# Layer 0 of a four-layer kernel: ten chunks of x turned twice instead of stored and loaded back

## The chip, the cores and the metric

The kernel runs on one core of a Trainium2 chip. The core has a matrix engine (TensorE, "PE" in the profile; "PEld" is its weight load), a vector engine (VectorE, DVE), an activation engine (ScalarE, ACT), a general engine (GpSimd, POOL) and a queue engine (SyncE, SP) that here only issues transfers. Each engine runs its own instruction stream in order; semaphores tie the streams together. SBUF is the on-chip memory of 128 partitions; PSUM is the small memory that TensorE writes into, eight banks of 512 fp32 values in each partition; transfers (DMA) go between SBUF and device memory (DRAM). The metric is the device time of one execution in microseconds. Everything is fp32.

## The reference, cut to what matters

Four residual layers on x of shape (1, 256, 256, 128), that is 65536 tokens of 128 channels. Each is `x = x + f(_gn(x))`, where `_gn` is a group norm whose means run over all tokens. Only the start of layer 0 is touched: the group statistics, and the LayerNorm row factors and the triangle bias that attention needs.

```python
def _gn(v, G=32, eps=1e-5):                      # mean and variance over all tokens and 4 channels
    g = v.reshape(B_, H_, W_, G, C_ // G)
    m = jnp.mean(g, axis=(1, 2, 4), keepdims=True)
    s = jnp.var(g, axis=(1, 2, 4), keepdims=True)
    return ((g - m) / jnp.sqrt(s + eps)).reshape(v.shape)

def _L0_conv_ref(x, mask, ...):                  # x is _gn(x) here
    xn = (x - mu) * jax.lax.rsqrt(var + EPS) * ln_w + ln_b        # LayerNorm of each token
    tri_bias = jnp.einsum('bijd,dh->bhij', xn, w_tri)[:, None]
    q, k, v = ...                                                  # xn @ w_q, w_k, w_v, 4 heads of 32
    scores = jnp.einsum('bimhc,binhc->bihmn', q, k) + tri_bias + mask_bias
    o = jnp.einsum('bihmn,binhc->bimhc', jax.nn.softmax(scores, axis=-1), v)
    return (sigmoid(xn @ w_g + b_g) * o) @ w_o + b_o

x = x + _L0_conv_ref(_gn(x), ...)
```

The bias `tri_bias` is shared by all rows of the attention, so attention can't start before every token of x has been through the LayerNorm sums, and these need the group statistics of all tokens first. So x is passed over twice before attention begins.

## The kernel before

x is cut into 32 chunks of 2048 tokens (`SC`, `NSC`), 1 MiB each. The input has tokens along the rows (`x_tok`); the layers want channels on the partitions (`xT`, a DRAM scratch tensor), so each chunk is turned by TensorE.

**First stage** (L262 to L380). `load0(i)` issues the load of the i-th chunk of `order0` into a buffer `p0_x` on SP. Three such buffers, and three more borrowed for the first six loads, bound how far it runs ahead: inside the loop the load of chunk i+3 is issued when chunk i has been turned. For each half of a chunk, 8 transposes go into a PSUM tile `p0_t` of two banks (L359), two `bn_stats` on VectorE sum it (L361), and ScalarE copies it to SBUF (L366), regrouping the tokens. Chunks 0 to 13 (`HELD` = 14) stay in SBUF; chunks 14 to 31 go to three buffers `p0_xc` and from there by SP to `xT` (L375). Of these, 14 to 16 (`FRESH` = 3) are the last three to use the buffers, and are still there at the end. `order0` is 17 to 31, 14 to 16, 0 to 13. From the seventh chunk on, each chunk also runs one step of `folds()`, small weight products on TensorE and VectorE that use weights loaded by POOL. Behind the last chunk but one comes an aggregate of all sums so far (`gn_part`, L380 and L181), behind the last one the small chain to the group mean and deviation (`gn_merge`, `gn_groups`).

**Second pass** (L437 to L592), order written out by hand (`manual_schedule`: program order is the order on every engine). Over `order` = 14, 15, 16, 0, 1, 2, 3, 17, 4, 18, 5, ... : `rows1(i)` squares the chunk on ScalarE (L452) and multiplies it by `wt` on TensorE (L455): four pieces of 512 tokens, each into its own 32 of the 128 columns of the array and so side by side. `squares1(i-1)` adds the products of the squares to the same PSUM tile (L463), and VectorE evicts it (L468). `turn1(i-2)` turns the evicted rows with four transposes (L476) into `p1_pt`, which has two buffers, and `keep1(i-2)` copies them to `raw` (L480). `marks` says at which iteration the variance, root and normalization of finished rows are done. `fetch()` issues the load of a stored chunk from `xT` into one of the three buffers (L396), and `keep()` the store of a held chunk to `xT` (L403): eight halves before the pass, the others at each iteration that uses a fetched chunk. At iterations 11 and 20 to 27 the first rows, loads and projections of attention are put in between (`first_rows`, `load_x`, `load_rs`, `first_qk`, `first_v`). PSUM is full: three banks for `p1_pr`, two for `p1_pt`, three for the pool `psP` of those small products.

**Attention** (from L598) then loads groups of 1024 tokens from `xT` and runs most of the first half of the span; nothing of it is changed.

Of the kernel before, what the change touches and what calls it, by code (L numbers as in the profile page):

```python
# [8 lines left out]
F32 = mybir.dt.float32  # L9
# [6 lines left out]
P = 128  # L16
# [15 lines left out]
def kernel(ctx: ExitStack, tc: tile.TileContext, a: dict, out: bass.AP):  # L32
# [214 lines left out]
    with tc.tile_pool(name="x0", bufs=1, reuse_waits="tile") as xres, tc.tile_pool(name="p0", bufs=3, reuse_waits="tile") as sb:  # L247
# [3 lines left out]
        def hold(s):  # L251
            if s < 4:
                held[s] = tuple(gt_tile(f"x0_{s}_{h}", *tags[2 * s + h]) for h in range(2))
            elif s < 9:
                tile_ = att_sb.tile([P, 2, GT], F32, name=f"x0_{s}", tag="qk" if s < 6 else "vg", bufs=2 if s < 6 else 3)
                held[s] = tile_.rearrange("p a t -> p (a t)")
            else:
                held[s] = xres.tile([P, SC], F32, name=f"x0_{s}")
            return held[s]

        order0 = [*range(HELD + FRESH, NSC), *range(HELD, HELD + FRESH), *range(HELD)]
        with tc.tile_pool(name="p0ps", bufs=3, space=PSUM, reuse_waits="tile") as ps, tc.tile_pool(name="f0ps", bufs=2, space=PSUM, reuse_waits="tile") as fps, tc.tile_pool(name="f0", bufs=1, reuse_waits="tile") as wk, tc.manual_schedule():  # L262
            xts, loaded = {}, {}

# [87 lines left out]
            nc.sync.dma_start(mk, a["L0_conv_mask"].rearrange("b (t p) n -> p (b t) n", p=P))  # L352
            for i, s in enumerate(order0):
                xt = xts.pop(s)
                xc = hold(s) if s < HELD else sb.tile([P, SC], F32, name="p0_xc", tag="xs")
                for c in range(2):
                    pt = ps.tile([P, 8, P], F32, name="p0_t")
                    for k in range(8):
                        nc.tensor.transpose(pt[:, k, :], xt[:, c, k, :], ident)  # L359
                    for h in range(2):  # L360
                        nc.vector.bn_stats(  # L361
                            stats0[:, i * 4 + 2 * c + h, :],
                            pt[:, 4 * h : 4 * h + 4, :].rearrange("p k n -> p (k n)"),
                        )
                    xh = xc[c] if isinstance(xc, tuple) else xc[:, c * GT : (c + 1) * GT]
                    nc.scalar.copy(  # L366
                        xh.rearrange("p (n k) -> p n k", k=8),
                        pt.rearrange("p k n -> p n k"),
                    )
                if i < 3:  # L370
                    load0(i + 6)
                elif i > 5:
                    load0(i + 3)
                if s not in held:
                    nc.sync.dma_start(xT[:, s * SC : (s + 1) * SC], xc)  # L375
                    loaded[s] = xc
                if i >= 6:
                    next(steps, None)
                if i == NSC - 2:
                    mv_first = gn_part(stats0, 0, T // CK - 4, "gn0_a")  # L380
# [1 line left out]


        fresh = range(HELD, HELD + FRESH)
        order = [*fresh, *range(4)]
        for i in range(HELD - 4):
            order += [HELD + FRESH + i, 4 + i]
        order += range(HELD + FRESH + HELD - 4, NSC)
        to_load, to_store = [s for s in order if s not in held and s not in fresh], list(held)
        loaded = {s: loaded[s] for s in fresh}  # L390

        def fetch():
            if to_load:
                s = to_load.pop(0)
                loaded[s] = sb.tile([P, SC], F32, name="p1_xc", tag="xs")
                nc.sync.dma_start(loaded[s], xT[:, s * SC : (s + 1) * SC])  # L396

        def keep():
            if to_store:
# [2 lines left out]
                    at += s * SC  # L402
                    nc.sync.dma_start(xT[:, at : at + xh.shape[-1]], xh)  # L403

        for _ in range(8):
            keep()
        mv0 = gn_merge(
            mv_first, gn_part(stats0, T // CK - 4, T // CK, "gn0_b"), 1.0 - 4.0 * CK / T, "gn0_mv"
# [25 lines left out]
        nc.vector.tensor_scalar(woh, wo, 0.5 * SHIFT, None, ALU.mult)  # L434


        with tc.tile_pool(name="p1", bufs=3, reuse_waits="tile") as wk_sb, tc.tile_pool(name="p1ps", bufs=3, space=PSUM, reuse_waits="tile") as ps, tc.tile_pool(name="p1pt", bufs=2, space=PSUM, reuse_waits="tile") as psT, tc.tile_pool(name="p1mm", bufs=3, space=PSUM, reuse_waits="tile") as psP:  # L437
# [3 lines left out]
            pw = psP.tile([P, 1], F32, name="p1_pw", tag="mm")  # L441
            for c in range(4):
                nc.tensor.matmul(pw[32 * c : 32 * c + 32, :], lhsT=mw, rhs=ones[:, 0:1], start=True, stop=True)
            nc.vector.tensor_copy(off, pw)
            with tc.manual_schedule():
                prs, trs, turned, sqs = {}, {}, {}, {}

                def rows1(i):
                    xc = held[order[i]] if order[i] in held else loaded[order[i]]
                    sqs[i] = sb.tile([P, SC], F32, name="p1_sq", tag="xt")  # L450
                    for at, xh in spans(xc):
                        nc.scalar.activation(sqs[i][:, at : at + xh.shape[-1]], xh, AF.Square, bias=mrneg, scale=r0)  # L452
                    prs[i] = ps.tile([P, CK], F32, name="p1_pr")
                    for c in range(4):
                        nc.tensor.matmul(  # L455
                            prs[i][32 * c : 32 * c + 32, :], lhsT=wt, rhs=piece(xc, c), start=True, stop=False
                        )

                def squares1(i):
                    pr = prs.pop(i)  # L460
# [40 lines left out]
                    )  # L501

                def first_rows():
                    pt = psP.tile([P, 2, P], F32, name="p1_rs", tag="mm")
# [30 lines left out]
                def first_qk():  # L535
                    tiles(0)
                    t = groups[0]
                    for j, what in enumerate("qk"):
                        pm = psP.tile([P, CK], F32, name="p1_mm", tag="mm")
                        nc.tensor.matmul(pm, lhsT=wf[:, j * D : (j + 1) * D], rhs=t["xn"][:, 0:CK], start=True, stop=True)  # L540
                        if j:
                            nc.vector.tensor_scalar(t["k"][:, 0:CK], pm, cqkg[:, 1:2], None, ALU.add)
                        else:
                            nc.vector.tensor_scalar(t["q"][:, 0:CK], pm, cqkg[:, 0:1], qscale, ALU.add, ALU.mult)

                def first_v():
                    t = groups[0]
                    pm = psP.tile([P, CK], F32, name="p1_mm", tag="mm")
                    for k in range(4):
                        nc.tensor.matmul(  # L550
                            pm[:, k * D : (k + 1) * D], lhsT=t["xn"][:, k * P : (k + 1) * P],
                            rhs=wf[:, 2 * D : 3 * D], start=True, stop=True,
                        )
                    nc.vector.tensor_tensor(t["v"][:, 0:4, :], pm.rearrange("p (k d) -> p k d", d=D), cv, ALU.add)

                qscale = 1.0 / float(HC) ** 0.5
                marks = {8: [(0, 4)], 17: [(4, 8), (14, 21)], 24: [(8, 12), (21, 25)], 29: [(12, 14), (25, 28)]}
                for i in range(NSC + 2):
                    if i < NSC:
                        rows1(i)  # L560
# [1554 lines left out]
```

## Time and profile before

| what | value |
|---|---|
| median of 3 runs | 3225.62 us (3222.66 to 3227.78) |
| the profiled execution, its own time | 3230.19 us |
| its span in the trace | 3228.1 us |
| mean granted TensorE clock | 0.973 |
| busy over the span: PE, DVE, ACT, POOL | 95%, 70%, 63%, 54% |
| first stage | 0 to 153.4 us |
| second pass, to attention's first scores | 153.4 to 244.2 us |
| moved by DMA in the first 140.3 us | 53.71 MB |
| moved by DMA from 153 to 247 us | 27.94 MB |

How to read it: the two stages changed take 7.6% of the span, and the whole-span shares say nothing about them; each stage is read from its own windows. A row of the timeline gives the start in us from the span's start, the busy time, the engine, the line of the kernel, the operation with the tiles that it writes and reads, how many instructions are merged into it, and in brackets how long the engine stood idle before and what ended that. A matrix product of fp32 shows as two records, so four products are x8. A row of a group gives busy time, mean ns of one, and the idle time before them with its releasers. The granted clock is the share of full speed that the throttle gave TensorE. DMA share is the mean busy share of the core's 16 DMA engines; it can come out a little over 1.

### The profile page before, as it was taken

The page shows a single profiled execution, that of the slowest core. Times are in us where ns is not written, and L with a number is a line of the kernel's source. Part 1 is how long each engine was busy: PE and PEld are TensorE (multiplying, and loading weights), DVE is VectorE, ACT ScalarE, POOL GpSimd, SP SyncE. Part 2 cuts the span into 40 slices and gives each one's busy share as a digit, 9 for nine tenths or more (in the row PEclk, how much of TensorE's full clock was granted, in tenths as well). Part 3 has the DMA queues.
Part 4 walks back from the last instruction along what each step waited for, and adds up shares of the span by engine and source line. Part 5 has one row for each costly group of instructions (what it writes and reads, how often), then busy time and mean ns, then how long its engine had stood idle before and what let it go on. Part 6 is the DMA issues. An engine that isn't in the chain of part 4 may idle for free. (4 is left out here: it accounts for less than half of the span.)

```text
span 3228.1 us, 51744 instructions
## 1 busy us (share of the span) xinstructions
PE 3052.8 (95%) x19916; PEld 1633.6 (51%) x19916; DVE 2260.7 (70%) x2631; ACT 2035.8 (63%) x2276; POOL 1741.9 (54%) x955
## 2 busy tenths in 40 slices
PE   5699999999999999998798899999999999979998
PEld 4535555555555555552533344444699943324444
DVE  5657888888888888884456454445455578867887
ACT  3577777777777777764477544444344457767776
POOL 4006777777777777772277000000255568848887
PEclk8899999999999999999899899999999999989999
DMA  9982333333333333349689677676699989986885
GB/s 377 397 302 96 110 123 114 106 114 118 113 112 120 113 107 116 118 149 418 190 306 390 248 294 301 238 266 257 262 351 351 351 332 387 386 287 198 236 236 156
DMA packets 289239, 746.16 MB, mean 231 GB/s; under 512 B 68314, under 2 KB 138860, under 8 KB 240700
## 3 DMA queue, kind: packets, MB, share of 16 engines
q1 hardware_dynamic: 276561, 716.84, 62.0%
q0 software_dynamic: 9136, 24.01, 2.0%
q8 instruction: 159, 2.61, 0.3%
q10 hardware_dynamic: 3288, 1.93, 0.2%
q14 instruction: 95, 0.77, 0.1%
HBM read 455.24 MB, written 287.45 MB: 230 GB/s over the span
## 5 line engine op out<-in xcount | busy, mean ns | idle before, releaser
L679 POOL TENSOR_TENSOR p_es<-p_e 128x1024 f32<-128x1024 f32 x256 | 603.1, 2366 | 319.0 <-DMA p_x<-xT 195.3
L669 DVE TENSOR_TENSOR p_e<-p_S,tri_raw 128x1024 f32<-128x1024 f32 x512 | 609.3, 1212 | 143.4 <-PE p_S L659 143.3
L677 ACT ACTIVATE p_e<-p_e,mbT 128x1024 f32<-128x1024 f32 x512 | 552.1, 1138 | 62.1 <-DVE p_e L669 62.0
L1273 PE MATMUL p_pm<-p_zn,wf 128*128 128x512 f32 x1040 | 450.4, 595 | 1.9 <-ACT p_a L1339 1.9
L644 PE MATMUL p_mm<-p_xn,w 128*128 128x512 f32 x764 | 404.4, 612 | 0.0
L1273 PEld LDWEIGHTS p_pm<-p_zn,wf 128*128 128x128 f32 x1040 | 197.4, 190 | 255.0 <-issue 248.1
L659 PE MATMUL p_S<-p_qk 32*128 32x256 f32 x4096 | 295.4, 400 | 3.3 <-DVE p_e L669 3.3
L1407 POOL MEMSET k<- 128x512 f32 x1 | 0.5, 526 | 517.1 <-PE p_pm L1273 517.1
L659 PEld LDWEIGHTS p_S<-p_qk 32*128 32x128 f32 x4096 | 186.0, 184 | 159.2 <-PE p_mm L635 91.7
L2073 PE MATMUL tp_z<-p_B,tp_at 128*128 128x256 f32 x1024 | 250.5, 388 | 1.1 <-DVE tp_at L2064 1.1
L692 PE MATMUL p_o<-p_e,p_vg 128*32 128x256 f32 x4096 | 248.8, 383 | 0.0
L626 POOL TENSOR_TENSOR p_xn<-p_xn,p_rs 128x1024 f32<-128x1024 f32 x62 | 148.9, 2401 | 180.8 <-DMA p_rb<-rzD 99.4
L1438 POOL TENSOR_TENSOR k<-k,p_sq 128x512 f32<-128x512 f32 x128 | 163.0, 1274 | 134.4 <-ACT p_sq L1436 134.3
L2073 PEld LDWEIGHTS tp_z<-p_B,tp_at 128*128 128x128 f32 x1024 | 185.3, 191 | 23.4 <-DVE tp_at L2064 1.9
L1437 DVE TENSOR_TENSOR k<-tp_z,k 128x512 f32<-128x512 f32 x128 | 88.5, 692 | 127.5 <-ACT p_sq L1436 127.5
L644 PEld LDWEIGHTS p_mm<-p_xn,w 128*128 128x128 f32 x764 | 125.1, 190 | 103.6 <-issue 87.3
L692 PEld LDWEIGHTS p_o<-p_e,p_vg 128*32 128x32 f32 x4096 | 120.4, 110 | 110.4 <-ACT p_vg L650 41.5
L650 ACT ACTIVATE p_vg<-p_mm,bgh 128x512 f32<-128x512 f32 x128 | 88.0, 687 | 135.0 <-PE p_mm L644 135.0
L1434 ACT COPY p_K<-tp_z 128x512 f32<-128x512 f32 x128 | 75.1, 586 | 155.3 <-PE tp_z L2073 155.3
L1343 DVE SCALAR_TENSOR_TENSOR p_b<-p_pm,b2w,p_b 128x1024 f32<-128x1024 f32 x64 | 82.2, 1284 | 125.2 <-PE p_pm L1273 111.2
L635 PEld LDWEIGHTS p_mm<-w,p_xn 128*128 128x128 f32 x1016 | 133.8, 192 | 61.3 <-issue 60.6
L648 ACT ACTIVATE p_qk<-p_mm,cqkg 128x512 f32<-128x512 f32 x127 | 87.5, 689 | 122.5 <-PE p_mm L644 122.2
(429 smaller groups left out, 6087.7 us busy)
## 6 DMA issues: line engine op xcount, KB each, us to landing
p_x<-x2T SPq DMA_DIRECT2D x57, 1024.0 KB
x<-x1T SPq DMA_DIRECT2D x47, 1024.0 KB
p_x<-in_x_dram SPq DMA_DIRECT2D x32, 1024.0 KB
p_x<-xT SPq DMA_DIRECT2D x64, 512.0 KB
p_rs<-rsD SPq DMA_DIRECT2D x64, 512.0 KB
x2T<-x SPq DMA_DIRECT2D x32, 1024.0 KB
aD<-p_a SPq DMA_DIRECT2D x32, 1024.0 KB
bD<-p_b SPq DMA_DIRECT2D x32, 1024.0 KB
```

Of the source, the lines that this page charges most:

```text
L626: nc.gpsimd.tensor_tensor(xn, xn, groups[g]["rs"], ALU.mult)
L635: nc.tensor.matmul(pm[:, k * D : (k + 1) * D], lhsT=t["xn"][:, b * P : (b + 1) * P], rhs=wf[:, 2 * D : 3 * D], start=True, stop=True,)
L644: nc.tensor.matmul(pm, lhsT=w, rhs=t["xn"][:, cs_], start=True, stop=True)
L659: nc.tensor.matmul(Ss[h // 2][:, h % 2, u, :], lhsT=t["k"][hp, r * N + u * P : r * N + (u + 1) * P], rhs=t["q"][hp, r * N : (r + 1) * N], ...
L669: nc.vector.tensor_tensor(e[:, :, 2 * p : 2 * p + 2, :].rearrange("p u h n -> p h u n"), Ss[p], triT[:, 2 * p : 2 * p + 2, :, :], ALU.add,)
L677: nc.scalar.activation(e[:, u, :, :], e[:, u, :, :], AF.Exp, bias=mbT[:, u, i : i + 1])
L679: nc.gpsimd.tensor_tensor(es, e[:, 0, :, :], e[:, 1, :, :], ALU.add)
L692: nc.tensor.matmul(t["o"][hp, r % 2, :], lhsT=t["v"][:, r * 2 + u, hp], rhs=e[:, u, h, :], start=(u == 0), stop=(u == 1),)
L1273: nc.tensor.matmul(pm[:, c, :], lhsT=wf2[:, i, :], rhs=zns[s][:, k * CK : (k + 1) * CK], start=True, stop=True)
L1437: nc.vector.tensor_tensor(k1, pz, k1, ALU.add)
L1438: nc.gpsimd.tensor_tensor(k2, k2, sq, ALU.add)
L2073: nc.tensor.matmul(pz[:, t, :], lhsT=at[:, u, t * P : (t + 1) * P], rhs=Bc[:, u, :], start=(u == 0), stop=(u == 1))
```

## The change

Ten chunks, 17 to 26 (`redo`), are no longer copied or stored in the first stage: they are loaded, turned and summed only. In the second pass they are loaded again from x, turned a second time by the new `remake(i + 1)` at the end of the iteration before their own, copied to SBUF (first half by ScalarE, second by VectorE), and stored to `xT` from there. `order0` mixes two such chunks with one of the stored chunks 27 to 31, and then the fresh with the held ones; `folds()` starts at the 11th chunk. The last five held chunks (9 to 13, `late`) are used right after the fresh ones and stored before the pass; their five buffers (`x0_9` to `x0_13`) then take the fetched chunks. Fetches and keeps have fixed iterations, `marks` and the attention pieces are moved, `p1_pt` has one buffer, and a pool of two tiles of two banks (`room()`) serves the second turning and the small products.

```diff
-                held[s] = xres.tile([P, SC], F32, name=f"x0_{s}")
+                held[s] = xres.tile([P, SC], F32, name=f"x0_{s}", tag=f"x0_{s}")
...
-        order0 = [*range(HELD + FRESH, NSC), *range(HELD, HELD + FRESH), *range(HELD)]
+        redo = range(HELD + FRESH, NSC - 5)
+        order0 = []
+        for k in range(5):
+            order0 += [*redo[2 * k : 2 * k + 2], NSC - 5 + k]
+        order0 += [14, 0, 1, 2, 3, 4, 15, 5, 6, 7, 8, 9, 16, 10, 11, 12, 13]
...
-                xc = hold(s) if s < HELD else sb.tile([P, SC], F32, name="p0_xc", tag="xs")
+                xc = None
+                if s not in redo:
+                    xc = hold(s) if s < HELD else sb.tile([P, SC], F32, name="p0_xc", tag="xs")
...
+                    if s in redo:
+                        continue
                     xh = xc[c] if isinstance(xc, tuple) else xc[:, c * GT : (c + 1) * GT]
                     nc.scalar.copy(
...
-                if s not in held:
+                if s not in held and s not in redo:
                     nc.sync.dma_start(xT[:, s * SC : (s + 1) * SC], xc)
                     loaded[s] = xc
-                if i >= 6:
+                if i >= 10:
                     next(steps, None)
...
-        order = [*fresh, *range(4)]
-        for i in range(HELD - 4):
-            order += [HELD + FRESH + i, 4 + i]
-        order += range(HELD + FRESH + HELD - 4, NSC)
-        to_load, to_store = [s for s in order if s not in held and s not in fresh], list(held)
+        late = range(HELD - 5, HELD)
+        order = [*fresh, *late]
+        for i in range(HELD - 5):
+            order += [i, HELD + FRESH + i]
+        order += range(HELD + FRESH + HELD - 5, NSC)
+        to_load, to_store = [*range(HELD + FRESH, NSC)], [*late, *range(HELD - 5)]
+        fetch_at = [5, 6, 7, 8, 9, 9, 11, 13, 15, 17, 19, 21, 23, 25, 26]
+        keep_at = [1, 2, 3, 4, 6, 8, 10, 12, 14]
...
         def fetch():
...
-                loaded[s] = sb.tile([P, SC], F32, name="p1_xc", tag="xs")
-                nc.sync.dma_start(loaded[s], xT[:, s * SC : (s + 1) * SC])
+            s = to_load.pop(0)
+            k = (s - HELD - FRESH) % 5
+            x = xres.tile([P, SC], F32, name="p1_x", tag=f"x0_{late[k]}")
+            if s in redo:
+                loaded[s] = x.rearrange("p (c k d) -> p c k d", c=2, d=D)
+                nc.sync.dma_start(
+                    loaded[s], x_tok[s * SC : (s + 1) * SC, :].rearrange("(c p k) d -> p c k d", p=P, k=8)
+                )
+            else:
+                loaded[s] = x
+                nc.sync.dma_start(x, xT[:, s * SC : (s + 1) * SC])
...
-        for _ in range(8):
+        for _ in late:
             keep()
...
-        with ... tc.tile_pool(name="p1pt", bufs=2, space=PSUM ...) as psT, tc.tile_pool(name="p1mm", bufs=3, space=PSUM ...) as psP:
+        with ... tc.tile_pool(name="p1pt", bufs=1, space=PSUM ...) as psT, tc.tile_pool(name="p1x", bufs=2, space=PSUM ...) as psX:
+            def room():
+                return psX.tile([P, 8, P], F32, name="p1_t")
...
+                def remake(i):
+                    s = order[i]
+                    if s in redo:
+                        x = loaded[s]
+                        loaded[s] = sb.tile([P, SC], F32, name="p1_xc", tag="xs")
+                        for c in range(2):
+                            pt = room()
+                            for k in range(8):
+                                nc.tensor.transpose(pt[:, k, :], x[:, c, k, :], ident)
+                            (nc.vector.tensor_copy if c else nc.scalar.copy)(
+                                loaded[s][:, c * GT : (c + 1) * GT].rearrange("p (n k) -> p n k", k=8),
+                                pt.rearrange("p k n -> p n k"),
+                            )
+                        nc.sync.dma_start(xT[:, s * SC : (s + 1) * SC], loaded[s])
...
-                marks = {8: [(0, 4)], 17: [(4, 8), (14, 21)], 24: [(8, 12), (21, 25)], 29: [(12, 14), (25, 28)]}
+                marks = {9: [(9, 17)], 17: [(0, 4), (17, 21)], 26: [(4, 9), (21, 25)], 29: [(25, 28)]}
                 for i in range(NSC + 2):
+                    for at in fetch_at:
+                        if i == at:
+                            fetch()
+                    if i in keep_at:
+                        keep()
                     if i < NSC:
                         rows1(i)
-                        if order[i] not in held:
-                            fetch()
-                            if i > 1:
-                                keep()
                     if i > 1:
                         turn1(i - 2)
                     if 0 < i <= NSC:
                         squares1(i - 1)
                     if i > 1:
                         keep1(i - 2)
+                    if i + 1 < NSC:
+                        remake(i + 1)
...
-                    if i == 11:
+                    if i == 20:
                         first_rows()
-                    if i == 20:
                         load_x(0)
+                    if i == 22:
                         load_rs(0)
-                    if i == 22:
+                    if i == 24:
                         normal_x(0)
                         load_x(1)
-                    if i == 24:
+                    if i == 25:
                         load_rs(1)
-                    if i == 26:
+                    if i == 27:
                         first_qk()
-                    if i == 27:
+                    if i == 28:
                         normal_x(1)
                         first_v()
```

More of the change, by code (lines that the diff above doesn't have):

```diff
@@ L384 @@
         fresh = range(HELD, HELD + FRESH)
-        order = [*fresh, *range(4)]
-        for i in range(HELD - 4):
-            order += [HELD + FRESH + i, 4 + i]
-        order += range(HELD + FRESH + HELD - 4, NSC)
-        to_load, to_store = [s for s in order if s not in held and s not in fresh], list(held)
+        late = range(HELD - 5, HELD)
[6 more added lines that the diff above has]
+        keep_at = [1, 2, 3, 4, 6, 8, 10, 12, 14]
         loaded = {s: loaded[s] for s in fresh}
         def fetch():
-            if to_load:
-                s = to_load.pop(0)
-                loaded[s] = sb.tile([P, SC], F32, name="p1_xc", tag="xs")
-                nc.sync.dma_start(loaded[s], xT[:, s * SC : (s + 1) * SC])
+            s = to_load.pop(0)
[9 more added lines that the diff above has]
+                nc.sync.dma_start(x, xT[:, s * SC : (s + 1) * SC])
         def keep():
@@ L434 @@
         nc.vector.tensor_scalar(woh, wo, 0.5 * SHIFT, None, ALU.mult)
-        with tc.tile_pool(name="p1", bufs=3, reuse_waits="tile") as wk_sb, tc.tile_pool(name="p1ps", bufs=3, space=PSUM, reuse_waits="tile") as ps, tc.tile_pool(name="p1pt", bufs=2, space=PSUM, reuse_waits="tile") as psT, tc.tile_pool(name="p1mm", bufs=3, space=PSUM, reuse_waits="tile") as psP:
+        with tc.tile_pool(name="p1", bufs=3, reuse_waits="tile") as wk_sb, tc.tile_pool(name="p1ps", bufs=3, space=PSUM, reuse_waits="tile") as ps, tc.tile_pool(name="p1pt", bufs=1, space=PSUM, reuse_waits="tile") as psT, tc.tile_pool(name="p1x", bufs=2, space=PSUM, reuse_waits="tile") as psX:
+            def room():
+                return psX.tile([P, 8, P], F32, name="p1_t")
             mw = wk_sb.tile([P, 32], F32, name="p1_mw", bufs=1)
             nc.vector.tensor_scalar(mw, wt, mneg, None, ALU.mult)
-            pw = psP.tile([P, 1], F32, name="p1_pw", tag="mm")
+            pw = room()[:, 0, 0:1]
             for c in range(4):
@@ L503, in first_rows @@
                 def first_rows():
-                    pt = psP.tile([P, 2, P], F32, name="p1_rs", tag="mm")
+                    pt = room()[:, 0:2, :]
                     for u in range(2):
@@ L538, in first_qk @@
                     for j, what in enumerate("qk"):
-                        pm = psP.tile([P, CK], F32, name="p1_mm", tag="mm")
+                        pm = room()[:, 0:4, :].rearrange("p k d -> p (k d)")
                         nc.tensor.matmul(pm, lhsT=wf[:, j * D : (j + 1) * D], rhs=t["xn"][:, 0:CK], start=True, stop=True)
@@ L547, in first_v @@
                     t = groups[0]
-                    pm = psP.tile([P, CK], F32, name="p1_mm", tag="mm")
+                    pm = room()[:, 0:4, :].rearrange("p k d -> p (k d)")
                     for k in range(4):
```

## The prediction

> **What bounds it now.** First the busy time by windows, to see which resource is full in each stage of layer 0. Columns: window, its length, busy us (and instructions) of PE, PEld, DVE, ACT, POOL, then granted clock, DMA share, GB/s.
>
> ```profile
> 20.00:103.00 83.00, 53.94 (x313) 48.17 (x312) 49.73 (x95) 34.92 (x36) 24.86 (x47) 0.78 1.02 406
> 103.00:136.00 33.00, 23.74 (x161) 21.05 (x160) 24.46 (x40) 19.78 (x20) 0.00 (x0) 0.84 0.96 375
> 120.00:140.00 20.00, 15.44 (x120) 12.95 (x119) 19.01 (x32) 15.38 (x16) 0.00 (x0) 0.99 1.02 390
> 161.00:204.00 43.00, 42.73 (x342) 14.10 (x338) 19.06 (x47) 35.09 (x23) 0.00 (x0) 1.00 0.95 373
> ```
>
> The first stage is held by transfers (share 0.96 to 1.02, PE half idle). The second pass is held by TensorE: 42.73 busy of 43.00, while the transfers, though also near full, keep nobody waiting there. Next the timeline where the stages meet, for what lies between the last loads and the second pass.
>
> ```profile
> 140.30 1.94 PE L359 MATMUL p_t<-ident,p_x 128*128 128x128 f32 x16 [1.33 <-DMA p_x<-in_x_dram]
> 143.93 3.52 DVE L181 BATCH_NORM_AGGREGATE gn_a<-stats 128x2 f32<-128x744 f32 x1
> 147.36 2.42 DVE L361 BATCH_NORM_STATS2 stats<-p_t 128x6 f32<-128x512 f32 x4
> 153.38 6.06 ACT L452 ACTIVATE p_sq<-p_xc,mrneg,gn_rstd 128x2048 f32<-128x2048 f32 x3 [0.47 <-DVE mrneg L414]
> ```
>
> The chunk before the last lands at 140.30; its sums, the 3.52 us aggregate and the last chunk's sums follow without a gap, and 13.1 us later the second pass begins. So that landing sets the end of the stage. Then one iteration of the second pass:
>
> ```profile
> 174.87 0.66 PE L476 MATMUL p_pt<-ident,p_tr 128*128 128x128 f32 x4
> 175.46 1.07 PE L463 MATMUL p_pr<-p_sq,slide 128*32 128x512 f32 x8
> 176.34 1.04 PE L455 MATMUL p_pr<-p_xc,wt 128*32 128x512 f32 x8
> 176.59 0.75 DVE L468 TENSOR_SCALAR p_tr<-p_pr,off 128x512 f32<-128x512 f32 x1 [1.61 <-PE p_pr L463]
> 177.26 0.25 DVE L480 COPY tri_raw<-p_pt 128x96 f32<-128x96 f32 x1
> 177.40 0.66 PE L476 MATMUL p_pt<-ident,p_tr 128*128 128x128 f32 x4
> ```
>
> PE goes round in 2.53 us: turns 0.59 to the next start, squares 0.88, row products 1.06. The last is 0.18 over the equal work of the squares: the turn at 177.40 waits for the eviction that ends at 177.34. Last, the prices of the moved work, from the timeline and the groups by form:
>
> ```profile
> 131.50 1.94 PE L359 MATMUL p_t<-ident,p_x 128*128 128x128 f32 x16 [0.76 <-DMA p_x<-in_x_dram]
> 135.19 1.01 ACT L366 COPY x<-p_t 128x1024 f32<-128x1024 f32 x1 [0.18 <-PE p_t L359]
> L285 DVE COPY mbT<-f_mk 128x512 f32<-128x512 f32 x1 | 0.7, 675 | 0.0
> L480 DVE COPY tri_raw<-p_pt 128x96 f32<-128x96 f32 x32 | 7.9, 248 | 0.6 <-PE p_pt L476 0.6
> ```
>
> **Stage 1: what goes.** Up to the landing at 140.30 the queues moved 53.7 MB: 31 loads and 18 stores of 1.05 MB, and some 2.3 MB of weights. Afterwards only chunks 14 to 16 and 27 to 31 are stored, and the store of 16 is issued behind the load of the chunk before the last: 7 stores instead of 18, 11.5 MB less. At 406 GB/s that is 28.4 us. Ends: 33 if the hole of 375 against 406 also closes, 22 if two holes of 3 us open, because a load is issued only when the transposes three chunks earlier are done, and no backlog of stores then feeds the queue. I take 28.5, nearest to the longest row. VectorE does not become the bound: 20 sums took 12.30 us in a dense run, 2.46 us a chunk; from 16.5 on, 31 chunks and some 10 us of folding work end at 103, ahead of 112. ACT loses 20 copies of 1.01 us; they waited on sums and transfers, worth nothing. The folding steps start at the 11th instead of the 7th chunk, the same instructions on PE, DVE and POOL's mask store. The seventh needs weights landing near 62 us, its chunk comes near then; zero taken, 3 us at most, since a late fold holds PE's transposes and with them the next load.
>
> **SP.** Ten stores of 0.33 us of issue move from its stage-1 order into the second pass. Each waits there for both copies, and the next fetch or keep is queued behind it; the ten reloads read x instead of xT, the same 1 MiB. The fetches run 1 to 9 iterations ahead. Total in the second pass: 15 fetches, 9 keeps, 10 stores and what is left of the 5 keeps issued at the end of stage 1, under 39 MiB, at 2.6 us each 101 us, inside its 126. The first remake needs chunk 17 about 23 us in; nine stores ahead of it, three of them moved before the pass starts, make it land near 17. Cover 6 us; without it PE waits for the excess. Taken: zero.
>
> **Second pass: what comes.** A remake at R puts 16 transposes on PE, 1.94 us. The first half is copied by ACT from R+1.12 for 1.01 us (the copy at 135.19 begins 1.12 after its transposes); the second by DVE, from R+2.00. No row has that DVE copy: from the copies of 512 and 96 columns the slope is 427 ns per 416, so 1024 cost 1.20 us, end R+3.20. The strided write is unknown on DVE; on ACT the same pattern costs 1.01, so I bound it by 1.01 and 1.28 (the dearest 1024 column DVE row here). The row products of the same chunk are next in PE's program order, so PE stands: two of the four pieces need the DVE half, start at R+3.26, and take 0.88, since the four run side by side in column groups: R+4.14, against 1.06 before. Price 3.08 each, ten: 30.8 us. The square of that chunk (2.09 on ACT) ends at R+5.4, its product starts near R+7.5: hidden. In DVE's order the copy follows the eviction and the row copy, done near R+1.1: free.
>
> The tile for turned rows has one buffer now. The turn must wait also for the copy that today ends 0.17 after the eviction (177.51 against 177.34); 22 iterations have no remake in between to hide it: 3.7 us. Second scratch pool: two buffers, each emptied two iterations earlier: zero.
>
> Moved marks: today's stalls of 1.75 us at 209 (a DVE block of 3.5 us) and 0.45 for the first rows fall into iterations with a remake and vanish; at the 29th, one block of 3.0 (normal), 1.28 and 0.68 delays the eviction, about 2.4 more. Net +0.3.
>
> Sum: -28.5 + 30.8 + 3.7 + 0.3 = +6.3 us. The profiled execution took 3230.19 (span 3228.1, 2.1 around it), so 3236.5 there; the median of the runs is 4.6 lower, 3225.62, so 3232.
>
> **A rule against it.** The windows row at 120 to 140 us holds 120 transposes at a granted clock of 0.99, 16 of them in 1.94 us. The Trainium skill (TensorE: Matmul & The Clock Gate, Part 4: PE-mode transpose) says that a transpose takes about 275 ns in a kernel and doesn't count as activity for the clock. Each row here does last 273 ns, but they overlap and start every 121 ns, and the clock stayed up. By the rule the 160 transposes would be an estimated 44 us, the sum some 25 us higher; the rows decide for 19.4.
>
> **Rivals.**
> 1. The evacuation is hidden: PE finds work or the copies end under the transposes. Then a remake costs 1.94 - 0.18 = 1.76, the pass +21.6, the change -6.9: 3219, faster. It decides below 1.8 us a remake. Against it: the program order puts the products directly behind the transposes.
> 2. Stage 1 gives more, 33 to 35: the hole near 118 us closes and half-speed transposes (clock 0.78 up to 103) no longer delay loads. Then +1: 3227. For it: less waiting keeps PE warmer. Against: only three load buffers.
> 3. Starvation: without stores queued behind them, loads leave holes in stage 1 (22 saved), or a fetch comes late in the second pass (6 to 9 us). Then +13 to +15, 3239 to 3241. For it: the 375 GB/s row lies where only loads remained. Against: 390 at full clock just after.
> 4. The stores are hidden in stage 1 anyway and nothing is saved: +35, 3260. The DMA share of 1.02 excludes it nearly.
>
> **How the numbers follow.** A run tells 0.2%, 6.5 us, from no change. The forecast, +3 to +11 around +6.3, lies across that bound: 0.40, of it 0.24 slower, 0.16 within. Rival 1: 0.18 (0.14 faster, 0.04 within). Rival 2: 0.20 (0.17 within, 0.03 faster). Rivals 3 and 4: 0.22, of it 0.21 slower. So faster 0.17, within 0.38, slower 0.45. Range 3217 (rival 1, a little more) to 3242 (rival 3); the forecast's own is 3228 to 3237.
>
> **What would show it.** The second pass should begin near 125 us instead of 153.4, and last about 126 us to attention's first scores instead of 91, so that these come near 250 instead of 244. An iteration pair with a remake should take 8.4 us instead of 5.05, with PE waiting for the DVE copy ahead of the row products. Wrong if that wait is missing, if fetches are waited for, or if the pass begins after 131.

## The result and the profile after

The changed kernel takes 3244.16 us (median of four runs, 3243.65 to 3247.18) against 3225.52 (3222.66 to 3227.78): a ratio of 1.0059 with a 95% interval of 1.0046 to 1.0072, so it is slower by 18.6 us. The forecast was 3232 and its range ended at 3242. The direction was right, the size was not.

Two moments divide the loss. The second pass began (first square on ACT) at 153.38 us and now begins at 134.37: 19.0 saved. The store of the first triangle bias, which follows attention's first scores, moved from 247.25 to 266.31: 19.06 lost. So the second pass, with the scores up to that store, grew by 38.1 us. The span grew by 17.3; 1.8 us came back in later stages, and where was not followed up. The two stores, before and after:

```profile
247.25 0.33 SPq L768 DMA_DIRECT2D triD<-tri_raw  x1
266.31 0.33 SPq L807 DMA_DIRECT2D triD<-tri_raw  x1
```

The start of stage 1 in the changed kernel, from its timeline (start, duration, engine, line and operation, count, idle time before and its releaser; an SPq row is SyncE issuing transfers):

```profile
25.64 7.66 SPq L383 DMA_DIRECT2D xT<-p_xc  x2
33.41 3.68 SPq L277 DMA_DIRECT2D p_x<-in_x_dram  x3
41.53 4.72 PE L365 MATMUL p_t<-ident,p_x 128*128 128x128 f32 x22 [4.84 <-DMA p_x<-in_x_dram]
```

The fourth to sixth chunk issue no load. The next one needs the buffer of the seventh chunk, whose transposes end only near 32.8, and stands on SyncE behind the store of chunk 28, which waits for an ACT copy that ends at 32.9. It goes out at 33.41; PE then stands for 4.84 us. The stage by windows (window, length, busy us and instructions of PE, PEld, DVE, ACT, POOL, then granted clock, DMA share, GB/s):

```profile
36.00:40.00 4.00, 0.69 (x7) 0.45 (x5) 3.00 (x6) 1.93 (x2) 3.16 (x7) 0.86 0.80 275
40.00:44.00 4.00, 2.47 (x12) 2.50 (x13) 0.49 (x1) 0.10 (x1) 2.17 (x5) 0.50 0.79 305
84.00:88.00 4.00, 4.00 (x24) 3.90 (x24) 2.37 (x4) 1.01 (x1) 0.00 (x0) 0.67 0.57 224
104.00:108.00 4.00, 4.00 (x24) 3.94 (x23) 2.15 (x4) 1.01 (x1) 0.00 (x0) 0.61 0.81 323
```

These are the holes. In the last two PE is busy throughout, but at a granted clock of 0.67 and 0.61: the chunk it turns has landed, its buffer comes free late, and the queues run short of loads. Each time PE had waited for a load just before (2.17 us at 83.33, 2.71 at 103.58), and in the next 4 us the clock is back at 1.00. Up to the landing of the chunk before the last, the changed kernel moved 42.5 MB in 119.36 us, 356 GB/s; the kernel before moved 53.7 MB in 140.30 us, 383 GB/s. Against 406 GB/s the one loses 14.7 us and the other 8.0. The end of the stage, from the timeline:

```profile
119.36 2.63 PE L365 MATMUL p_t<-ident,p_x 128*128 128x128 f32 x16 [0.24 <-DMA p_x<-in_x_dram]
123.68 3.51 DVE L181 BATCH_NORM_AGGREGATE gn_a<-stats 128x2 f32<-128x744 f32 x1
125.59 3.65 PE L365 MATMUL p_t<-ident,p_x 128*128 128x128 f32 x16 [3.60 <-DMA p_x<-in_x_dram]
134.37 4.08 ACT L473 ACTIVATE p_sq<-p_xc,mrneg,gn_rstd 128x2048 f32<-128x2048 f32 x2 [0.47 <-DVE mrneg L432]
```

Before, the last chunk had been there by the time the aggregate ended, and 13.1 us lay between the landing before it and the pass. Now it lands at 125.59, its transposes run at half speed (3.65 us against 1.94), and 15.0 us lie between. So 20.9 us saved at the landing become 19.0 at the pass.

One iteration with a chunk that is turned again, from the timeline:

```profile
182.60 0.63 PE L512 MATMUL p_pt<-ident,p_tr 128*128 128x128 f32 x4 [0.27 <-DVE tri_raw L516]
184.16 1.97 PE L488 MATMUL p_t<-ident,p_x 128*128 128x128 f32 x16
185.28 1.01 ACT L489 COPY p_xc<-p_t 128x1024 f32<-128x1024 f32 x1 [2.05 <-PE p_t L488]
186.16 1.23 DVE L489 COPY p_xc<-p_t 128x1024 f32<-128x1024 f32 x1 [0.95 <-PE p_t L488]
186.35 2.14 PE L476 MATMUL p_pr<-p_xc,wt 128*32 128x512 f32 x8 [0.23 <-ACT p_xc L489]
187.44 0.14 PEld L476 LDWEIGHTS p_pr<-p_xc,wt 128*32 128x32 f32 x4 [0.94 <-DVE p_xc L489]
188.42 0.66 PE L512 MATMUL p_pt<-ident,p_tr 128*128 128x128 f32 x4
```

From turn to turn it takes 5.82 us where the kernel before took 2.53. With R = 184.16 the copies begin at R+1.12 and R+2.00, the last products at R+3.28, the next turn at R+4.26. The weight load at 187.44 names the cause: 0.94 us of waiting for DVE's copy. The tail of the pass:

```profile
253.14 0.63 PE L512 MATMUL p_pt<-ident,p_tr 128*128 128x128 f32 x4 [2.22 <-DVE tri_raw L516]
253.70 1.78 PE L499 MATMUL p_pr<-p_sq,slide 128*32 128x512 f32 x8
255.23 1.96 PE L476 MATMUL p_pr<-p_x,wt 128*32 128x512 f32 x8
```

A block on DVE, the normalisation of finished rows and behind it two pieces of attention (1.28 and 0.68 us), stops PE for 2.22 us, and the next two groups run at about half speed (1.78 and 1.96 us, 1.06 otherwise; granted clock 0.59 from 253.14 to 257.20). No instruction of the pass's chunks waits for a fetch.

### The profile page after: what moved, and what is told of

Same layout as the page of the kernel before. It is cut to its first block, busy times and chain, and to the rows that moved or that the text cites. A ratio compares the mean times of both kernels' runs of the same rounds, so it can differ in the third digit from the quotient of the medians.

```text
span 3245.4 us, 52041 instructions
## 1 busy us (share of the span) xinstructions
PE 3073.5 (95%) x20076; PEld 1644.0 (51%) x20076; DVE 2271.2 (70%) x2635; ACT 2025.0 (62%) x2265; POOL 1742.4 (54%) x955
```

## The experiments

Medians of the kernel before differ between the sets of runs (3225.5 to 3229.3), so times are compared as ratios to the kernel before of the same set, or inside one set. Pass lengths run from the first row products on PE to attention's first scores: 90.7 us before (153.55 to 244.23), 128.75 in the changed kernel (134.53 to 263.28). Each kernel has one trace, and the end of stage 1 differs between traces of the same stage-1 code: row products start at 153.55 in the kernel before and at 157.33 in e3, where stage 1 is the same; at 134.53, 134.37 and 133.65 with the stage of the changed kernel; at 127.54 to 129.07 with the edit of e1 added. So 1.5 us, or 4 for the kernel before, in where the stage ends in one trace shows nothing by itself.

### Are the holes in stage 1 the missing load buffers? (e1_deep_loads)

```diff
-                    if 3 <= i < 6:
+                    if i < 18 and i % 6 > 2:
                         xts[s] = att_sb.tile([P, 2, 8, D], F32, name="p0_x", tag="vg", bufs=3)
...
-                if i < 3:
+                if i < 15:
                     load0(i + 6)
-                elif i > 5:
+                elif i > 17:
                     load0(i + 3)
```

> The changed kernel, with six load buffers instead of three for the first 21 loads (the three tiles lent by chunks 6 to 8 are used three times instead of once). Theory: the first stage saved 19.0 us instead of 28.5 because loads are issued too late and leave the transfer queue empty (windows of 275, 305, 224 and 323 GB/s). Then the holes before about 90 us go: the second pass begins 5 to 8 us earlier than 134.4, the time falls to 3236 to 3239. Rival: the stage is held by TensorE at half clock and by VectorE's sums, the holes only follow; then the start stays within 2 us of 134.4 and the time near 3244.

Measured: 3237.93 us, ratio 1.004 (1.0028 to 1.0052). The first row products start at 127.84 instead of 134.53: 6.7 us earlier. The windows of this run:

```profile
36.00:40.00 4.00, 2.78 (x24) 2.35 (x23) 3.98 (x8) 1.14 (x2) 2.31 (x6) 1.00 1.04 395
40.00:44.00 4.00, 2.77 (x24) 2.33 (x22) 3.65 (x7) 0.89 (x1) 3.10 (x6) 1.00 1.02 413
60.00:64.00 4.00, 2.55 (x12) 2.13 (x12) 2.33 (x7) 2.02 (x2) 0.00 (x0) 0.50 1.03 415
84.00:88.00 4.00, 3.79 (x18) 3.82 (x19) 1.40 (x3) 0.34 (x1) 0.00 (x0) 0.50 0.75 298
```

Where six buffers were used, the hole near 40 us is gone; where the loop is back at three, the hole at half clock is still there. From 20 to 83 us the queues moved 403 GB/s instead of 376. The missing buffers are shown as the cause of the early holes. Half clock by itself is not: at 60 to 64 us it is at 0.50 here, and with six buffers the queues still move 415 GB/s. The last load still came late: PE waited 4.34 us for it.

### Is it the wait for DVE's copy that makes a remake dear? (e2_early_remake)

```diff
                     if i < NSC:
                         rows1(i)
+                    if i + 1 < NSC:
+                        remake(i + 1)
                     if i > 1:
                         turn1(i - 2)
                     if 0 < i <= NSC:
                         squares1(i - 1)
                     if i > 1:
                         keep1(i - 2)
-                    if i + 1 < NSC:
-                        remake(i + 1)
```

> The changed kernel, with the second turning of the next chunk put directly behind the row products of the present one, so that the four turns and the squares' products (0.6 + 0.9 us on TensorE) stand between the transposes and the products that need the copies. Theory: of the 3.5 us that a remake costs, 1.3 to 1.4 us are TensorE standing for the copies; they go, and with them part of the 0.2 us wait of the turn: a pair of iterations falls from 8.6 to about 7.0 us, the time by 13 to 17 us to 3227 to 3231. Rival: the wait only moves, to the squares of the remade chunk on ScalarE; the pair stays above 8 us and the time above 3238.

Measured: 3229.53 us, ratio 1.0007 (0.9994 to 1.002); first scores at 247.88, 15.4 us earlier, with the pass starting at the same time. Its timeline:

```profile
177.92 1.97 PE L488 MATMUL p_t<-ident,p_x 128*128 128x128 f32 x16
179.72 0.60 PE L512 MATMUL p_pt<-ident,p_tr 128*128 128x128 f32 x4
179.93 1.23 DVE L489 COPY p_xc<-p_t 128x1024 f32<-128x1024 f32 x1 [1.81 <-PE p_t L488]
181.14 1.12 PE L476 MATMUL p_pr<-p_xc,wt 128*32 128x512 f32 x8
184.87 1.97 PE L488 MATMUL p_t<-ident,p_x 128*128 128x128 f32 x16
```

Turn and squares now lie between the transposes and the products, and cover the copies. The pair of iterations takes 6.95 us (177.92 to 184.87) instead of the changed kernel's mean of 8.63; 6.95 against the 5.05 of the kernel before leaves 1.90 for a remake, close to the transposes alone (1.80 to the next start). This is the prediction's first rival, but it needs this edit.

### What does the second turn buffer's loss cost alone? (e3_one_turn_buffer)

The kernel before, with one edit:

```diff
-tc.tile_pool(name="p1pt", bufs=2,
+tc.tile_pool(name="p1pt", bufs=1,
```

> The kernel before, with one buffer instead of two for the turned rows (p1_pt) and nothing else. Theory: each iteration of the second pass waits 0.2 us longer for the row copy, 32 times: an iteration goes from 2.53 to about 2.75 us, the time up by 5 to 7 us to 3231 to 3233. Rival: the wait is hidden by the eviction that the turn waits for anyway; no change.

Measured: 3230.84 us, ratio 1.0014 (1.0002 to 1.0026). The pass from its first square to the first scores is 96.87 us against 90.85, so 6.0 longer. Two iterations in its timeline:

```profile
180.18 0.63 PE L476 MATMUL p_pt<-ident,p_tr 128*128 128x128 f32 x4 [0.27 <-DVE tri_raw L480]
182.94 0.63 PE L476 MATMUL p_pt<-ident,p_tr 128*128 128x128 f32 x4 [0.27 <-DVE tri_raw L480]
```

The iteration takes 2.76 us instead of 2.53: 0.23, not the 0.17 of the sum. Some 26 iterations of the pass are longer by that, and 26 by 0.23 is the 6.0.

### What is stage 1 worth alone? (e4_stage1_alone)

The first stage of the changed kernel and the second pass of the kernel before. The ten chunks are not turned a second time: the pass loads them unturned, and a plain copy of them goes into xT during attention, so this part of the computation is left out.

```diff
-        order0 = [*range(HELD + FRESH, NSC), *range(HELD, HELD + FRESH), *range(HELD)]
+        redo = range(HELD + FRESH, NSC - 5)
...
+                    if s in redo:
+                        continue
...
-                if s not in held:
+                if s not in held and s not in redo:
...
+                if s in redo:
+                    src = x_tok[s * SC : (s + 1) * SC, :].rearrange("(p k) d -> p (k d)", p=P)
```

> The first stage of the changed kernel with the second pass of the kernel before. Left out: the ten chunks are neither turned again nor stored turned; the second pass loads them unturned from x and uses them as they are, and a plain copy of them goes to xT during attention, so the output is not the reference's. Theory: the first stage's whole saving shows, the second pass starts near 134.4 us and lasts 91 us as before: 3206 to 3208, 18 to 20 us below before. Rival: the saving on the clock is less than the earlier start, because the second pass of before has less transfer time behind it; 3212 or more.

Measured: 3208.61 us, ratio 0.9938 (0.992 to 0.9956), so 20 us faster. From its timeline:

```profile
124.37 3.65 PE L365 MATMUL p_t<-ident,p_x 128*128 128x128 f32 x16 [4.29 <-DMA p_x<-in_x_dram]
133.31 1.06 PE L466 MATMUL p_pr<-p_xc,wt 128*32 128x512 f32 x1 [0.94 <-DVE wt L428]
```

The pass starts 20.2 us earlier than before and keeps its old length (133.31 to 223.61, 90.3). So the first half of the change is worth some 20 us, all of which reaches the end; and its price of 38 us lies in the second pass.

### Do the two costs add? (e6_deep_early)

The edits of e1 and e2 together.

> Both edits that paid alone, in the changed kernel: six load buffers for the first 21 loads, and each chunk turned again directly behind the row matmuls of the chunk before. Theory (the two costs lie in different stretches, stage 1 and the second pass, so they add): the pass starts near 127.5 us, the first scores come near 241 to 242, and the time is 6 to 7 us under that of the early turning alone (3229.5): 3222 to 3224, which is 2 to 5 us under the kernel before. Rival (the pass gives the gain back, because the chunks it fetches are no earlier when it starts earlier): a wait for a DMA shows in the pass, first scores at 246 to 248, time 3228 to 3230.

Measured: 3222.44 us, ratio 0.9988 (0.9979 to 0.9998). Products start at 129.07, first scores come at 242.25. From 1.0059, the edits alone took 0.0019 and 0.0052; 1.0059 less both is 0.9988. Each ratio is known to some 0.001; within that they add.

### A second turn buffer paid for with a row buffer (e7_two_turn_buffers)

e6, and

```diff
-tc.tile_pool(name="p1ps", bufs=3, ...) as ps, tc.tile_pool(name="p1pt", bufs=1, ...
+tc.tile_pool(name="p1ps", bufs=2, ...) as ps, tc.tile_pool(name="p1pt", bufs=2, ...
```

> The kernel with both edits, and two buffers of PSUM for the turned rows in place of one, paid for with one of the three buffers of the rows themselves. Theory (each turn in a plain iteration waits 0.22 to 0.27 us for DVE's copy of the turn before, and the remake's iterations now hold such a wait too): the plain iteration goes from 2.75 to about 2.5 us, the pass is 4 to 6 us shorter, the time 4 to 6 us under that of the run with both edits: 3217 to 3220. Rival (the third row buffer was needed: the row matmuls of a chunk then wait for DVE's addition of the chunk before the last): the waits move from the turn to the row matmuls, pass and time within 1.5 us of the run with both edits, or above.

Measured: 3248.14 us, ratio 1.0059 (1.0045 to 1.0073), 25.7 us over e6 in the same set. The rival held, and far more strongly than it was put. From the timeline:

```profile
179.62 1.07 PE L476 MATMUL p_pr<-p_xc,wt 128*32 128x512 f32 x8 [0.97 <-DVE p_tr L504]
183.14 1.06 PE L476 MATMUL p_pr<-x,wt 128*32 128x512 f32 x8 [0.87 <-DVE p_tr L504]
```

With two row buffers, a chunk's row products need the buffer that DVE has just begun to empty: PE stands 0.87 to 0.97 us in nearly every iteration, where it stood 0.27 for the turn. The pass is 137.0 us against 113.2. Taking the buffer from the turned rows, as the change does, was the cheap choice.

### Spreading the normalisation (e8_spread_marks, e13_marks_alone, e10_deep_early_marks)

One edit, on top of e7, of the changed kernel and of e6:

```diff
-26: [(4, 9), (21, 25)], 29: [(25, 28)]}
+23: [(4, 7), (21, 24)], 26: [(7, 9), (24, 25)], 29: [(25, 28)]}
```

> As the run with two turn buffers, and the normalisation of chunks 4 to 8 and 21 to 24 is split: 4 to 6 and 21 to 23 at iterations 23 to 25, the rest at 26 to 28. Theory (the block on DVE at iteration 28 holds up the turn by 2.2 us, and the half clock behind it costs one to two more): the wait of 2.2 us is gone or under 0.8, first scores and time 2 to 4 us earlier. Rival (DVE is as busy at iterations 25 and 28 together, the wait only moves, or two turn buffers have taken it already): within 1 us.

Measured on e7: 3242.09 us, ratio 1.0046 (1.0032 to 1.006), against 1.0059; the wait of 2.22 us is gone and the first scores are 3.7 us earlier, 0.95 of it because that pass began earlier. Because e7 had spoilt every iteration, the edit was run again on the changed kernel itself:

> The changed kernel with one edit: the normalisation of chunks 4 to 8 and 21 to 24, which runs at iterations 26 to 28, is split in two, one half at 23 to 25. This prices the block on DVE at iteration 28 by itself. Theory (the turn's wait of 2.2 us there, and the half clock of the two chunks behind it, are an own part of the loss): the wait of 2.2 us is gone, the first scores come 2 to 5 us earlier than 263.3, time 3239 to 3242. Rival (the DVE work is only moved and lengthens the iterations 23 to 25 by as much): within 1.5 us of the changed kernel's 3244.

Measured: 3241.55 us, ratio 1.0038 (1.0023 to 1.0053). First scores at 259.96, pass 126.31 us against 128.75. The total time alone would not settle it, since the two intervals overlap; the pass does, and the third run gives the same number.

> Six load buffers, the early turning and the split normalisation together, with the three row buffers and the one turn buffer of the changed kernel. Theory (the three costs lie in different stretches and add): first scores near 238 to 240, time 3217 to 3220, which is 6 to 9 us under the kernel before. Rival (the split only paid where two row buffers made DVE late in every iteration): within 1.5 us of the run with both edits, 3222.4.

Measured: 3220.94 us, ratio 0.9977 (0.9968 to 0.9987): faster than both kernels, and 8.4 us under the kernel before in its set. The pass is 110.72 us against 113.18 in e6: 2.46 less, where e13 gave 2.44. In both runs 0.82 us is left of the wait of 2.22, and the groups behind it take 1.04 to 1.07 us.

### Why is the last load late? (e9_earlier_16, e12_late_keeps)

In the changed kernel the last load is issued 0.5 us behind the store of chunk 16 and 0.4 ahead of the kept chunks' stores. The edit of e8 (on e7), and

```diff
-order0 += [14, 0, 1, 2, 3, 4, 15, 5, 6, 7, 8, 9, 16, 10, 11, 12, 13]
+order0 += [14, 0, 1, 2, 3, 4, 15, 5, 6, 16, 7, 8, 9, 10, 11, 12, 13]
```

> As the run with split normalisation, and chunk 16, which is stored in stage 1, is placed three chunks earlier, so that the last load is not issued behind its store. Theory (the last load is late because it queues behind this store's wait for the ACT copy): the last load lands 1 to 2 us earlier against the load before it, and the pass starts 1 to 2 us earlier. Rival (it lands late because it shares the memory with the five stores of kept chunks issued 0.4 us behind it): the last load's landing and the pass start move by less than 0.5 us.

Measured: 3243.76 us, ratio 1.0052 (1.0038 to 1.0066), no gain. The products start 1.2 us later, no more than traces of one stage differ. Another hole opened: from 113 to 116 us the queues moved 153 GB/s. The last load was issued only at 112.77, where e8 has 108.67, and landed at 119.19 (e8: 119.53), so 6.4 us after its issue instead of 10.9. The run therefore tests neither theory nor rival. The trace of e8 bounds the theory: the last load waits for the buffer of a chunk whose transposes end at 108.19, and goes out at 108.67, so the store took 0.5 us at most.

e10, with the five stores of kept chunks put on ACT's queue:

```diff
         for _ in late:
-            keep()
+            keep(nc.scalar)
```

> As the run with the three edits, and the five stores of kept chunks that are issued right behind the last load are issued from ACT's queue, behind its last copy. Theory (the last load is late because it shares the memory with these five stores): the last load lands 2 to 4 us earlier, the pass starts and the time is 2 to 3 us earlier. Rival 1 (the last load was not held up by them): pass start within 0.7 us. Rival 2 (the stores are then late, and the fetches that need their tiles with them): the pass starts earlier and waits for a DMA at its first chunks to be turned, time the same or later.

Measured: 3225.55 us, ratio 0.9989 (0.9979 to 0.9998), 4.6 us worse than e10. The edit did not do what it was to do. Three of the five stores left ACT before the last load had landed (107.35, 112.48, 118.54). SyncE, rid of the five, went straight on to the next kept chunks and issued their eight half stores from 111.72, behind the last load at 110.27. From its timeline:

```profile
111.72 16.90 SPq L421 DMA_DIRECT2D xT<-x  x8
124.91 3.52 PE L365 MATMUL p_t<-ident,p_x 128*128 128x128 f32 x16 [7.00 <-DMA p_x<-in_x_dram]
```

The last load landed 14.6 us after its issue instead of 10.1. The queues ran at 420 GB/s from 110 to 125 us, 6.3 MB, and no more than 2 or 3 MB of loads were open in that time; the rest were stores. That fits a last load which shares the memory with stores, but no run had it without stores behind it, so what this costs stays open.

### Would the kernel before gain from deeper loads as well? (e11_before_deep)

The edit of e1 in the kernel before.

> The kernel before with six load buffers for its first 21 loads, nothing else. It tells whether loading ten chunks twice pays by itself or only carries edits that would have paid without it. Theory (the kernel before stores after every chunk, its memory is busy between the loads, and it loses only 8 us of stage 1 against the best rate, most of it at its ends): pass start within 2 us of 153.4, time within 2 us of the kernel before. Rival (its loads run dry as well): pass start 4 to 7 us earlier, time 3219 to 3222, as good as the change with the same edit.

Measured: 3226.34 us, ratio 0.9992 (0.9982 to 1.0001); products start at 152.38 instead of 153.55. The pass began where the theory put it, and the time is 3 us lower where it allowed 2, an interval that reaches from 6 us lower to nothing: deeper loads give little there, where a store follows each of the first 18 chunks. In the same set e10 took 3220.94, 5.4 us less. So a kernel that turns ten chunks twice can be faster than before, but only with the repairs. What the second turning itself is worth stays open: e6 stands at 0.9988, not apart from the 0.9992 here, and from e6 to e10 it is the normalisation that was spread, which the kernel before never had.

## Why the prediction was wrong

**Stage 1, -28.5; measured -19.0. This is the step that failed.** The bytes were nearly right: 11.2 MB less up to the landing (53.7 against 42.5) where 11.5 were put, worth 0.9 us. The rate was not. The step wrote that "a load is issued only when the transposes three chunks earlier are done, and no backlog of stores then feeds the queue", priced that as two holes of 3 us, and then still took 28.5, "nearest to the longest row". But that row, 406 GB/s, was measured while stores stood in the queue behind every chunk; it priced the stage with the very cover that the change takes away. The holes cost 6.7 us more than those of the kernel before (14.7 less 8.0), and e1 gave about as much back with load buffers alone, although its later holes stayed. Another 1.9 us are the last load, which the step had not looked at: it took for granted that the chunk before the last sets the end, as in the kernel before. The upper end of 33 does not follow from its row either: 33 us at 375 instead of 406 GB/s are worth 2.5 us, so 31.

**Rival 3 was the right mechanism in its first half.** It put the stage at 22 saved. Of the 3 us still missing, 1.9 are the last load and 0.9 the bytes; its two holes of 3 us were nearly the 6.7 measured. Its second half, a late fetch, did not occur: the sum's zero for SyncE and the fetches was right.

**Rival 2 had the clock right and the loads wrong.** The prediction spoke of half-speed transposes only as a gain that rival 2 might bring. The clock did rise: the kernel before had 0.80 from 20 to 140 us, the changed kernel 0.90 from 20 to 120. But the queues moved 395 GB/s there and 366 here. In these traces the rate went with what stood in the queue, not with the clock.

**The remake, 3.08 each; measured 3.29.** The wait is where it was put, and DVE's copy took 1.23 us against 1.20 from the slope. (What the prediction calls its strided write is in the code a read of PSUM in steps of 512 bytes; the write is dense.) Twice 0.12 was missed: the next turn starts at R+4.26 and not R+4.14, and squares that are followed by transposes take 1.00 to the next start and not 0.88. Ten times 0.21 is 2.1 us. e2 shows the wait as the cause.

**One turn buffer, 0.17; measured 0.22 in plain iterations (2.75 against 2.53).** Over 22 of them 1.1 us more than the sum had.

**The marks, +0.3 net.** The block of about 2.4 us was there, and e13 and e10 took 2.44 and 2.46 us off by spreading it. The net was not measured by itself.

Together the pass was to grow by 34.8 us and grew by 38.1; 2.1 and 1.1 make 3.2 of the 3.3 between. The stage missed by 9.5. From the forecast of +6.3 these 12.8 lead to +19.1 at the bias store; the 17.3 of the span is that, less the 1.8 that later stages gave back, and the medians differ by 18.6.

**The rule on transposes.** The groups of the second turning in the changed kernel (busy us, mean ns of one, idle time before):

```profile
L488 PE MATMUL p_t<-ident,p_x 128*128 128x128 f32 x160 | 19.7, 276 | 0.0
L489 DVE COPY p_xc<-p_t 128x1024 f32<-128x1024 f32 x10 | 12.3, 1225 | 8.6 <-issue 6.0 <-PE p_t L488 2.5
```

The 160 transposes were busy 19.7 us, 123 ns each, as the rows of before had it (19.4). The Trainium skill (TensorE: Matmul & The Clock Gate, Part 4: PE-mode transpose) would have them at an estimated 44; its 275 ns is the mean of one record here too, 276, but the records overlap.

**What was foreseen of the traces.** Pass start near 125 (134.4), its length 126 (128.9), first scores near 250 (263.3), a pair of iterations 8.4 (8.63). "Wrong if [...] the pass begins after 131" named the place of the error.

## What to carry to other kernels

A transfer rate read from a stage belongs to the queue that stood in it. If a change takes stores out of the queue, count how many loads can be open at each moment, and price the stage with that (here 403 GB/s with six buffers and 376 with three, over the same 63 us); deeper load buffers may have to come with the change. Work that one engine produces, another copies and the first consumes is priced by the whole way round unless other work is put between in program order: moving one call a few lines up was worth 15 us here. And before a buffer is moved from one tile to another, see which of the two is emptied later.

## What the runs showed that was not expected

- How long PE waits for a load does not tell by itself whether it is slow behind it. In the changed kernel a wait of 2.17 us at 83.33 was followed by 16 transposes in 3.55 us, but one of 2.74 at 78.37 by 16 in 1.94. After 3.60 (there) and 4.34 (e1) they took 3.65; after 2.43 in e4 (at 118.14), 3.12 in e12 (at 115.98) and 3.91 in e6 (at 121.53) they took 1.94. The Trainium skill (TensorE: Matmul & The Clock Gate, Why this matters for your kernels) advises against gaps of more than about 3 us between bursts; here the clock was lost after a shorter gap and kept after longer ones. What else decides was not followed up.
- DVE's copy of 128x1024 fp32 out of PSUM, read in steps of 512 bytes as the code has it, took 1.225 us in the mean of ten, near what the slope of its plain copies gives (1.20); the step cost next to nothing that can be seen. ACT's took 1.016.
- Two row buffers instead of three, and two turn buffers instead of one, cost 0.77 us in a plain iteration (3.52 against 2.75), 24 us over the pass: the dearest single edit of this study was one that moved a buffer of 2 KB a partition.
